# Graph attention on one core: scores dealt to row groups, transposed by TensorE, summed over heads by VectorE

## The chip, the cores and the metric

The kernel runs on one core of a Trainium2 chip. The metric is the device time of one execution in microseconds (us). The kernel before takes 5000.75 us, the median of three runs (4999.63 to 5002.16).

## What is computed

One layer of graph attention with 12,500 nodes of 128 features and 412,500 edges, followed by two layer norms. The part that the change touches is the attention score of an edge: eight heads, each with its own bias and leaky ReLU, whose mean goes into one softmax over all edges.

```python
h = node_features @ Wn + bn
q, k, v = (node_features @ W + b for W, b in ((Wq, bq), (Wk, bk), (Wv, bv)))
eh = edge_features @ We + be
attn_in = jnp.concatenate([q[src], k[tgt], eh], axis=-1)
hmid = jax.nn.leaky_relu(attn_in @ A1 + b1, SLOPE)          # 128 wide, per edge
scores = jax.nn.leaky_relu(hmid @ A2 + b2, SLOPE)           # 8 heads, per edge
w = jax.nn.softmax(scores.mean(axis=-1), axis=0)            # over all edges
out = jax.ops.segment_sum(w[:, None] * v[tgt], src, num_segments=num_nodes)
y = layernorm(h + out) * gamma + beta
result = layernorm(x + y)                                   # without gain
```

## The kernel before, in words

The edges arrive sorted by target and must be summed by source. The kernel cuts them into 403 groups of 1024 edges and the groups into six **parts** (51, 62, 73, 73, 73 and 71 groups). It does two things at once.

**Making records** (`make`, L770). For each group TensorE forms the edge's 256-wide record (key and edge terms, and the value) by one-hot products (`rows`, L878 and L884), ScalarE copies it out of PSUM (`evacuate`, L895), and POOL writes each tile of 128 records to its place in a table in HBM by an indirect DMA (L907, 3224 of them, eight to a group). The place is counted by VectorE and TensorE (L809 to L860). Records are bucketed by the block of source nodes, 98 blocks in all.

**Summing units** (`sums_of`, L1004). A unit is two blocks of one part, so there are 49 units to a part and 294 in all. A unit holds 10 tiles of 128 records in the first part, 12 in the second and 14 in the other four. The records of a part can be read only when all of the part's groups are written, so the units of part p are summed while the records of part p + 1 are made, and the 49 units of the last part after the last record is written. The order is written out by hand: `sums_of` gives every function of a unit a step, and the loop at L1625 deals the steps evenly between the pieces of `make`. Nothing is reordered afterwards: each engine runs its instructions in that order.

A unit goes through these functions. `load` (L1037) reads its records `rt` from HBM into one of six buffers. `sources` (L1059) forms the local source index `sl` on VectorE, `turn` (L1068) transposes it on TensorE, `turned` (L1075) makes bytes of it (`slT`), `put` (L1082) writes them to HBM and `spread` (L1087) reads them back to all partitions as `rowB`: two DMAs, one after the other. With `rowB`, `onehot` (L1096) makes one-hot rows of four tiles at a time, `hidden` (L1105) adds the query term by products and the record's term by transposes (L1110) in PSUM, and `sloped` and `leaky` (L1130 on ScalarE, L1134 on VectorE) leave the hidden layer in the SBUF tile `hm`, 128 features by 14 times 128 edges.

Then come the functions that the change touches. `scores` (L1141) multiplies `hm` by the 128x8 weight, padded to 32 columns, in up to four **row groups**: tiles 0 to 3 of a unit of 14 go to partitions 0 to 31 of one PSUM bank, tiles 4 to 7 to partitions 32 to 63, 8 to 11 to the third and the last two to the fourth. The fourth group is shorter, so `biased` (ScalarE, L1162) and `leaky_scores` (VectorE, L1170) work in two pieces: 96 partitions by 512 columns and 32 by 256 (96 by 384 and 32 by 128 with 10 tiles, a single 128 by 384 with 12). `heads` (L1172) sums the heads and brings the edges back to partitions in one step: four products (three with 10 or 12 tiles) with the scores as the stationary operand and a 128x4 matrix of ones, `headsum`, as the moving one. They land in the first 14 columns of a PSUM bank `psS`. `maxima` (L1186) adds the mask and takes the maximum per partition, `maximum` (L1197) brings the 128 maxima to all partitions by a product with the identity, `reference` (L1205) takes the unit's maximum, `weights` (L1216) the exponentials. `select`, `weigh` and `add` (L1224 to L1274) sum the weighted values by source in other columns of the same bank, `total` (L1276) adds them to what the earlier parts gave, and `store` writes them.

PSUM has one bank `psc`, shared by `turn` and `scores`, and two banks `psm`, one to a unit, which `total` frees. After the last unit, `closing` norms the nodes.

Of the kernel before, what the change touches and what calls it, by code (L numbers as in the profile page):

```python
# [10 lines left out]
FP = mybir.dt.float32  # L11
# [9 lines left out]
P = 128  # L21
D = 128
DE = 64
H = 8
# [423 lines left out]
def sorted_path(  # L448
# [256 lines left out]
    empties(np_)  # L705
    A2s = const.tile([D, 32], FP)
    b2_c = const.tile([P, 1], FP)
    headsum = const.tile([P, 4], FP)

    def heads_consts():  # L710

        nc.vector.memset(A2s, 0.0)
        nc.sync.dma_start(out=A2s[:, :H], in_=A2)
        nc.vector.memset(b2_c, 0.0)
        nc.vector.memset(headsum, 0.0)
        for j in range(4):
            nc.sync.dma_start(out=b2_c[32 * j : 32 * j + H, :], in_=b2)
            nc.vector.memset(headsum[32 * j : 32 * j + 32, j : j + 1], 1.0)

    def spans():  # L720

# [282 lines left out]
    def sums_of(bp):  # L1004
# [129 lines left out]
            nc.vector.tensor_tensor(hm, ph[:, : n * P], hm, op=ALU.max)  # L1134


        def slices(m):
            sw = -(-m // 4)
            return sw, [(j, min(sw, m - j)) for j in range(0, m, sw)]

        def scores(i, t0, m):  # L1141
            st = state[i]
            sw, sl = slices(m)
            hm = st["hm"].pop(t0)
            psc = pscp.tile([P, 4 * P], FP, name="psc")
            for q, (j, n) in enumerate(sl):
                nc.tensor.matmul(  # L1147
                    psc[32 * q : 32 * q + 32, : n * P], A2s, hm[:, j * P : (j + n) * P],
                    start=True, stop=True,
                )  # L1150
            full = sum(n == sw for _, n in sl)
            st["z"] = psc, [(0, 32 * full, sw)] + [
                (32 * q, 32 * q + 32, n) for q, (_, n) in enumerate(sl) if q >= full
            ]

        def biased(i):
            st = state[i]
            psc, pieces = st["z"]
            z = zp_.tile([P, 4 * P], FP, name="z")
            st["z"] = z, pieces  # L1160
            for p0, p1, n in pieces:
                nc.scalar.activation(  # L1162
                    z[p0:p1, : n * P], psc[p0:p1, : n * P], AF.Identity, bias=b2_c[p0:p1, :]
                )

        def leaky_scores(i):
            z, pieces = state[i]["z"]
            for p0, p1, n in pieces:
                zs = z[p0:p1, : n * P]
                nc.vector.scalar_tensor_tensor(zs, zs, SLOPE, zs, op0=ALU.mult, op1=ALU.max)  # L1170

        def heads(i, t0, m):  # L1172
            st = state[i]
            sw, sl = slices(m)
            if t0 == 0:
                st["psS"] = psmp.tile([P, 4 * P], FP, name="psm")
            z = st.pop("z")[0]
            for j in range(sw):
                nv = sum(n > j for _, n in sl)
                nc.tensor.matmul(  # L1180
                    st["psS"][:, t0 + j : t0 + j + (nv - 1) * sw + 1 : sw],
                    z[: 32 * nv, j * P : (j + 1) * P], headsum[: 32 * nv, :nv],
                    start=True, stop=True,
                )

        def maxima(i):  # L1186

            st, nt = state[i], plans[i][0]
            st["S"] = scp.tile([P, TM], FP, name="S")
            nc.vector.scalar_tensor_tensor(  # L1190
                st["S"][:, :nt], st["sl"][:, :nt], 0.0, st["psS"][:, :nt],
                op0=ALU.min, op1=ALU.add,
            )
            st["mx"] = scp.tile([P, 1], FP, name="mx")
# [2 lines left out]
        def maximum(i):  # L1197

            st = state[i]
            psS = st["psS"]  # L1200
            nc.tensor.matmul(
                psS[:, :P], st.pop("mx").to_broadcast([P, P]), ident, start=True, stop=True
            )

        def reference(i):  # L1205
# [549 lines left out]
```

## Time and profile before

| | |
|---|---|
| median of three runs | 5000.75 us |
| the profiled execution's own time | 4997.18 us |
| its span, first to last instruction | 4995.4 us |
| busy: TensorE (PE), VectorE (DVE) | 4185.0, 3984.1 us |
| busy: ScalarE (ACT), GpSimd (POOL) | 3260.1, 3315.9 us |
| mean granted TensorE clock | 0.906 |

PE is TensorE's products and PEld its weight loads, which run beside them; DVE is VectorE, ACT ScalarE, SP the queue that issues most DMAs. A row of the table of groups gives line, engine, operation and tiles with their shape, the count, then busy time and the mean duration in ns, and behind a bar the idle time of the engine just before such instructions with what ended it. A float32 product stands in the trace as two products and two weight loads (the 1078 products of L1180 are 2156 rows), a transpose as one. The chain of waits follows the last instruction back, at each step to what released it; its rows give start, duration and what ran.

### The profile page before, as it was taken

How to read it: one execution, taken by the hardware profiler on the slowest of the kernel's cores; microseconds unless marked ns; L12 is line 12 of the kernel's file. 1: busy time of each engine (PE TensorE's matmuls, PEld its weight loads, DVE VectorE, ACT ScalarE, POOL GpSimd, SP SyncE). 2: the span in 40 equal slices, each digit the busy share in tenths (PEclk: the TensorE clock that was granted, in tenths of full speed). 3: DMA queues.
4: the chain of work that ended last, by engine and by line, in shares of the span. 5: the costliest groups of instructions: out<-in, count | busy, mean ns of one | idle time of the engine just before them, and what ended most of it. 6: DMA issues, size and time to landing. Idle time of an engine off the chain costs nothing.

```text
span 4995.4 us, 98371 instructions
## 1 busy us (share of the span) xinstructions
PE 4185.0 (84%) x32676; PEld 3106.9 (62%) x32676; DVE 3984.1 (80%) x10117; ACT 3260.1 (65%) x8686; POOL 3315.9 (66%) x3268
## 2 busy tenths in 40 slices
PE   5665488898888888899999899999899999899980
PEld 3443366676566666577676676676677766667760
DVE  8886477788777777788888888888888888677778
ACT  3433266666566666677677677777777777677876
POOL 5777777777777777777777777777777777310002
PEclk7776588899999999999999899999999999999995
DMA  8999699998999988899899898989899999788763
GB/s 287 360 349 347 237 327 340 347 301 269 307 322 334 324 294 289 281 318 310 309 307 311 297 322 313 311 305 314 285 329 313 321 318 309 251 291 278 263 224 142
DMA packets 604241, 1505.50 MB, mean 301 GB/s; under 512 B 103587, under 2 KB 315702, under 8 KB 601929
## 3 DMA queue, kind: packets, MB, share of 16 engines
q1 hardware_dynamic: 448681, 1069.47, 64.9%
q0 software_dynamic: 154752, 429.39, 22.7%
q8 instruction: 259, 4.24, 0.3%
q14 instruction: 261, 2.14, 0.1%
q10 hardware_dynamic: 288, 0.26, 0.0%
HBM read 929.49 MB, written 608.37 MB: 308 GB/s over the span
## 4 chain that ended last, share of the span: by engine, by line
DMA 35%; PE 23%; DVE 15%; POOL 12%; issue 7%; ACT 6%; SPq 1%; ACTq 0%; DVEq 0%; POOLq 0%
DMA rtab<-rec,idx 17%; POOL rtab L907 12%; DMA rt<-rtab 8%; PE psm L1271 6%; DMA row<-slT 4%; PE ph L1119 4%; DMA rowB<-row 3%; PE pkv L884 3%; PE ph L1110 3%; ACT rec L895 2%; PE psc L1147 2%; DVE hm L1134 2%; PE pkv L878 2%; ACT ohw L1242 2%; PE psm L1180 2%
## 5 line engine op out<-in xcount | busy, mean ns | idle before, releaser
L907 POOL DMA_INDIRECT rtab<-rec,idx x3224 | 3253.2, 1009 | 1046.2 <-issue 778.6
L895 ACT ACTIVATE rec<-pkv 128x1024 f32<-128x1024 f32 x806 | 821.9, 1020 | 876.0 <-DMA rtab<-rec,idx 550.4
L1242 ACT ACTIVATE ohw<-ohs,w 128x128 f32<-128x128 bf16 x3822 | 1258.4, 399 | 44.7 <-DVE ohs L1228 34.3
L1271 PE MATMUL psm<-rt,ohw 128*128 128x128 f32 x7644 | 1160.2, 294 | 9.7 <-ACT ohw L1242 9.3
L1271 PEld LDWEIGHTS psm<-rt,ohw 128*128 128x128 f32 x7644 | 999.1, 200 | 58.7 <-ACT ohw L1242 16.8
L1130 ACT ACTIVATE hm<-ph 128x512 f32<-128x512 f32 (+1 forms) x1078 | 581.5, 539 | 403.9 <-PE ph L1119 399.8
L1119 PE MATMUL ph<-ohT,qs 128*128 128x256 bf16 (+3 forms) x4116 | 819.7, 321 | 0.0
L878 PE MATMUL pkv<-kvs,ohd 128*128 128x256 bf16 x3224 | 532.0, 292 | 263.4 <-ACT rec L895 252.8
L1134 DVE TENSOR_TENSOR hm<-ph,hm 128x512 f32<-128x512 f32 (+1 forms) x1078 | 668.4, 620 | 102.6 <-ACT hm L1130 101.4
L1110 PE MATMUL ph<-ident,rt 128*128 128x128 f32 x3822 | 628.1, 283 | 44.5 <-DVE hm L1134 43.2
L884 PE MATMUL pkv<-WeS,eat 64*128 64x128 f32 x6448 | 635.6, 320 | 0.0
L884 PEld LDWEIGHTS pkv<-WeS,eat 64*128 64x128 f32 x6448 | 469.8, 205 | 191.7 <-issue 187.3
L1099 DVE TENSOR_SCALAR ohT<-rowB,iotaP 128x512 bf16<-128x512 uint8 (+1 forms) x1078 | 518.7, 481 | 85.4 <-DMA rowB<-row 80.6
L878 PEld LDWEIGHTS <-ohd 128*128 128x128 bf16 x3224 | 317.1, 103 | 388.0 <-issue 298.2
L1110 PEld LDWEIGHTS ph<-ident,rt 128*128 128x128 f32 x3822 | 472.5, 152 | 62.0 <-DVE hm L1134 51.2
L1228 DVE TENSOR_TENSOR ohs<-iotaE,sl 128x512 bf16<-128x512 bf16 (+1 forms) x1078 | 430.0, 399 | 68.3 <-ACT ohw L1242 66.4
L1119 PEld LDWEIGHTS <-qs 128*128 128x128 bf16 x4116 | 396.0, 100 | 128.7 <-issue 5.1
L847 DVE TENSOR_TENSOR ats<-pc,oh 128x792 f32<-128x792 f32 x403 | 392.2, 973 | 86.6 <-PE pc L829 82.7
L1180 PE MATMUL psm<-headsum,z 128*128 128x4 f32 (+1 forms) x2156 | 285.7, 254 | 135.7 <-DVE part L1287 88.3
L1147 PE MATMUL psc<-hm,A2s 128*32 128x512 f32 (+3 forms) x2352 | 341.1, 545 | 65.7 <-DVE slT L1078 62.1
L858 DVE TENSOR_REDUCE pos<-ats 128x8 f32<-128x792 f32 x403 | 390.0, 968 | 4.0
L1180 PEld LDWEIGHTS psm<-headsum,z 128*128 128x128 f32 (+1 forms) x2156 | 280.0, 201 | 156.8 <-DVE part L1287 105.9
(175 smaller groups left out, 4082.3 us busy)
## 6 DMA issues: line engine op xcount, KB each, us to landing
rt<-rtab SPq DMA_DIRECT2D x196, 1820.0 KB
eat<-in_ea SPq DMA_DIRECT2D x201, 512.0 KB
rt<-rtab SPq DMA_DIRECT2D x49, 1560.0 KB
rt<-rtab SPq DMA_DIRECT2D x49, 1300.0 KB
qs<-qtab SPq DMA_DIRECT2D x294, 192.0 KB
rtab<-rec,idx POOLq DMA_INDIRECT x3224
dstb<-dtab SPq DMA_DIRECT2D x201, 256.0 KB
rtab<-empty SPq DMA_DIRECT2D x98, 520.0 KB
```

The lines of the kernel that those rows point to most:

```text
L878: nc.tensor.matmul(pk[:, h, i, :], ohd[:, t * P : (t + 1) * P], kvs, start=(i == 0), stop=False,)
L884: nc.tensor.matmul(pk[:, h, i, :D], eat[h * DE : (h + 1) * DE, (j + i) * P : (j + i + 1) * P], WeS[h * DE : (h + 1) * DE, :], start=False, ...
L895: nc.scalar.activation(rec[:, :, :, : 2 * D], pk, AF.Copy)
L907: one_tile = nc.gpsimd.indirect_dma_start(out=rtab[p % TABS][:, :], out_offset=bass.IndirectOffsetOnAxis(ap=idxs[g][:, t : t + 1], axis=0) ...
L1099: nc.vector.tensor_scalar(st["oh"][k][:, : n * P], st["rowB"][:, t0 * P : (t0 + n) * P], iotaP, None, op0=ALU.is_equal,)
L1110: nc.tensor.matmul(ph[:, j * P : (j + 1) * P], st["rt"][:, t0 + j, :D], ident, is_transpose=True, start=(j == 0), stop=False,)
L1119: nc.tensor.matmul(ph[:, cols], st["qs"][:, j0 // t, s, :], oh[:, cols], start=False, stop=(s == 2 and j1 == t0 + n),)
L1130: nc.scalar.activation(hm, state[i]["ph", k][:, : n * P], AF.Copy, scale=SLOPE)
L1134: nc.vector.tensor_tensor(hm, ph[:, : n * P], hm, op=ALU.max)
L1180: nc.tensor.matmul(st["psS"][:, t0 + j : t0 + j + (nv - 1) * sw + 1 : sw], z[: 32 * nv, j * P : (j + 1) * P], headsum[: 32 * nv, :nv], sta ...
L1242: nc.scalar.activation(ohw[:, j, :], ohs[:, :, j], AF.Copy, scale=st["w"][:, t0 + j : t0 + j + 1])
L1271: nc.tensor.matmul(st["psS"][:, (1 + u) * P : (2 + u) * P], ohw[:, j, :], st["rt"][:, t0 + j, D : 2 * D], start=(k == 0), stop=(k == t - 1),)
```

## The change

Tile t of a unit now goes to row group t mod 4 and column block t div 4, so `scores` reads every fourth tile of `hm`. Where a group has a tile less than the others, an extra product fills its last block with a copy of the group's first tile, so that the four groups are equally wide, and `biased` and `leaky_scores` work on one piece of 128 partitions. `heads` transposes each block of 128 columns against the identity, and its output now takes 32 columns of `psS` per tile. `maxima` first sums the eight heads of each tile with a reduction of VectorE that reads PSUM, and then adds the mask from SBUF. `maximum` is the same operation marked as a transpose. `headsum` goes, with its five memsets.

```diff
         def scores(i, t0, m):
             st = state[i]
-            sw, sl = slices(m)
-            hm = st["hm"].pop(t0)
+            hm = st["hm"].pop(t0).rearrange("d (t e) -> d t e", e=P)
             psc = pscp.tile([P, 4 * P], FP, name="psc")
-            for q, (j, n) in enumerate(sl):
+            to = psc.rearrange("r (j e) -> r j e", e=P)
+            w = -(-m // 4)
+            for q in range(4):
+                n = len(range(q, m, 4))
                 nc.tensor.matmul(
-                    psc[32 * q : 32 * q + 32, : n * P], A2s, hm[:, j * P : (j + n) * P],
-                    start=True, stop=True,
-                )
+                    to[32 * q : 32 * q + 32, :n, :], A2s, hm[:, q:m:4, :], start=True, stop=True
+                )
+                if n < w:
+                    nc.tensor.matmul(
+                        to[32 * q : 32 * q + 32, n:w, :], A2s, hm[:, q : q + 1, :],
+                        start=True, stop=True,
+                    )
...
         def biased(i):
...
-            for p0, p1, n in pieces:
-                nc.scalar.activation(
-                    z[p0:p1, : n * P], psc[p0:p1, : n * P], AF.Identity, bias=b2_c[p0:p1, :]
-                )
+            nc.scalar.activation(z[:, :w], psc[:, :w], AF.Identity, bias=b2_c)
 
         def leaky_scores(i):
-            z, pieces = state[i]["z"]
-            for p0, p1, n in pieces:
-                zs = z[p0:p1, : n * P]
-                nc.vector.scalar_tensor_tensor(zs, zs, SLOPE, zs, op0=ALU.mult, op1=ALU.max)
+            z, w = state[i]["z"]
+            nc.vector.scalar_tensor_tensor(
+                z[:, :w], z[:, :w], SLOPE, z[:, :w], op0=ALU.mult, op1=ALU.max
+            )
 
         def heads(i, t0, m):
...
-            for j in range(sw):
-                nv = sum(n > j for _, n in sl)
+            for j in range(-(-m // 4)):
+                k = 32 * min(4, m - 4 * j)
                 nc.tensor.matmul(
-                    st["psS"][:, t0 + j : t0 + j + (nv - 1) * sw + 1 : sw],
-                    z[: 32 * nv, j * P : (j + 1) * P], headsum[: 32 * nv, :nv],
-                    start=True, stop=True,
+                    st["psS"][:, j * P : j * P + k], z[:k, j * P : (j + 1) * P], ident[:k, :k],
+                    is_transpose=True, start=True, stop=True,
                 )
 
         def maxima(i):
...
+            nc.vector.tensor_reduce(
+                st["S"][:, :nt],
+                st["psS"].rearrange("p (t r) -> p t r", r=32)[:, :nt, :H], AX.X, ALU.add,
+            )
             nc.vector.scalar_tensor_tensor(
-                st["S"][:, :nt], st["sl"][:, :nt], 0.0, st["psS"][:, :nt],
+                st["S"][:, :nt], st["sl"][:, :nt], 0.0, st["S"][:, :nt],
                 op0=ALU.min, op1=ALU.add,
             )
...
             nc.tensor.matmul(
-                psS[:, :P], st.pop("mx").to_broadcast([P, P]), ident, start=True, stop=True
+                psS[:, :P], st.pop("mx").to_broadcast([P, P]), ident,
+                is_transpose=True, start=True, stop=True,
             )
```

The order in which the functions are called is the same. What stands on the engines is shown at three places of a unit of 14 tiles of the last part, where only sums are left. A row is a line, an operation, output <- inputs and the output's shape; a float32 product is one row here.

First TensorE at `heads`, before the change: `z` is the scores, `headsum` the matrix of ones, and the row behind them is the transposes of `hidden`.

```order
L1071 MATMUL psc<-identB,sl 14x128
L1271 MATMUL psm<-rt,ohw 128x128 x4
L1180 MATMUL psm<-headsum,z 128x4 x2
L1180 MATMUL psm<-headsum,z 128x3 x2
L1110 MATMUL ph<-ident,rt 128x128 x2
```

The same place after the change (lines have moved: L1110 is now L1107, L1271 is L1266):

```order
L1068 MATMUL psc<-identB,sl 14x128
L1266 MATMUL psm<-rt,ohw 128x128 x4
L1171 MATMUL psm<-ident,z 128x128 x3
L1171 MATMUL psm<-ident,z 128x64
L1107 MATMUL ph<-ident,rt 128x128 x2
```

Four products with few columns have become four transposes at the same place.

Second TensorE at `scores` and `maximum`, before the change, where `A2s` is the padded weight and `mx` the maxima:

```order
L1119 MATMUL ph<-ohT,qs 128x512
L1147 MATMUL psc<-hm,A2s 32x512 x3
L1147 MATMUL psc<-hm,A2s 32x256
L1201 MATMUL psm<-ident,mx 128x128
L1271 MATMUL psm<-rt,ohw 128x128 x4
```

And after the change:

```order
L1116 MATMUL ph<-ohT,qs 128x512
L1142 MATMUL psc<-hm,A2s 32x512 x2
L1142 MATMUL psc<-hm,A2s 32x384
L1146 MATMUL psc<-hm,A2s 32x128
L1142 MATMUL psc<-hm,A2s 32x384
L1146 MATMUL psc<-hm,A2s 32x128
L1195 MATMUL psm<-ident,mx 128x128
L1266 MATMUL psm<-rt,ohw 128x128 x4
```

Four products have become six, and the extra product of the third group stands ahead of the fourth group's own. `maximum` stands where it stood.

Third VectorE at `maxima`, before the change: `slT` is what `put` writes, `ohs` the one-hot of `select`, `S` the sums with the mask, and the last row is the last piece of `hm`, which the unit's scores need.

```order
L1078 TENSOR_SCALAR slT<-psc 14x128
L1228 TENSOR_TENSOR ohs<-iotaE,sl 128x128x2
L1190 SCALAR_TENSOR_TENSOR S<-sl,psm 128x14
L1195 TENSOR_REDUCE mx<-S 128x1
L1099 TENSOR_SCALAR ohT<-rowB,iotaP 128x512
L1134 TENSOR_TENSOR hm<-ph,hm 128x256
```

And after the change:

```order
L1075 TENSOR_SCALAR slT<-psc 14x128
L1223 TENSOR_TENSOR ohs<-iotaE,sl 128x128x2
L1180 TENSOR_REDUCE S<-psm 128x14
L1184 SCALAR_TENSOR_TENSOR S<-sl,S 128x14
L1189 TENSOR_REDUCE mx<-S 128x1
L1096 TENSOR_SCALAR ohT<-rowB,iotaP 128x512
L1131 TENSOR_TENSOR hm<-ph,hm 128x256
```

The reduction stands behind `turned` and ahead of the last piece of `hm`. Elsewhere on VectorE and ScalarE the second row of L1170 and of L1162 is gone from units of 10 and 14 tiles; POOL and SP have the rows that they had.

19 lines of the change are left out of this document (4 added, 15 removed).

## The prediction

> **What bounds the kernel now.** I read the page's groups first, then busy time by stage, then the chain of waits inside two stages. The stages are cut where the POOL queue starts, where the first units are summed (640), where the last record is written (4303), where the chain changes its kind (4573) and where TensorE ends (4860).
>
> ```profile
> L907 POOL DMA_INDIRECT rtab<-rec,idx x3224 | 3253.2, 1009 | 1046.2 <-issue 778.6
> L907 POOL DMA_INDIRECT rtab<-rec,idx x3224: 957/963/1824, 31.3 to 4302.8; - x190
> core 0: us, PE busy (x) PEld busy (x) DVE busy (x) ACT busy (x) POOL busy (x), PEclk, DMA share, GB/s
> 31.00:640.00 609.00, 368.36 (x2071) 245.19 (x2071) 447.56 (x992) 229.06 (x516) 447.56 (x450) 0.70 0.94 323
> 640.00:1300.00 660.00, 571.48 (x4517) 423.60 (x4517) 510.49 (x1292) 414.03 (x1101) 498.22 (x493) 0.90 0.93 315
> 1300.00:4303.00 3003.00, 2718.88 (x22135) 2035.99 (x22133) 2476.67 (x6069) 2104.06 (x5588) 2306.68 (x2283) 0.96 0.91 309
> 4303.00:4573.00 270.00, 238.52 (x1770) 180.52 (x1770) 191.55 (x513) 188.49 (x555) 30.69 (x15) 0.96 0.83 284
> 4573.00:4860.00 287.00, 277.87 (x2143) 213.99 (x2142) 221.46 (x660) 236.83 (x702) 0.00 (x0) 0.99 0.70 247
> POOL rtab L907 <- issue: 553.6, 1815, 0.3
> ```
>
> *Up to 4303 the POOL queue is the bound.* From 1300 to 4303 it issues 2283 indirect DMAs in 3003 us, one in 1.315 us: 1.010 us of work (2306.68 / 2283) and a pause of 0.30 us that no other engine ends. The longest single pause there is 0.3 us, so POOL never waits for anyone. TensorE is busy for nine tenths of that stage and still has room. A faster PE, DVE or ACT gains nothing here; only a shorter issue does. The median issue is 0.963 us and the mean 1.009, so some are lengthened.
>
> *From 4303 to 4573 a round trip of two DMAs is the bound.* The next rows are the chain of waits there (start, duration, what):
>
> ```profile
> 4406.85 0.69 DVE hm L1134
> 4407.53 0.18 DVE slT L1078
> 4407.72 0.03 DVE ohs L1228
> 4407.75 5.32 DMA row<-slT
> ...
> 4413.13 4.55 DMA rowB<-row
> ...
> 4417.71 0.03 DVE ohT L1099
> ...
> 4418.79 0.19 DVE slT L1078
> ```
>
> The byte rows of one unit go to HBM (5.32 us) and come back (4.55 us), VectorE makes the first one-hot, a piece of `hm` and then the next unit's byte rows, which go the same way: 11.26 us from one `slT` to the next, with TensorE idle in between. Nothing in that ring is changed.
>
> *From 4573 to 4860 TensorE is the bound.* It is busy for 278 of 287 us, and the chain runs through it alone:
>
> ```profile
> 4690.52 0.89 PE psm L1271 x8
> 4691.41 0.44 PE ph L1110 x4
> 4691.85 0.65 PE ph L1119 x3
> 4692.50 0.99 PE psc L1147 x5
> 4693.48 0.42 PE psm L1201 x2
> ...
> 4698.83 0.95 PE psm L1180 x8
> ...
> 4700.38 0.89 PE psm L1271 x8
> ```
>
> One unit takes 9.86 us here, of which the changed lines have 0.99 + 0.42 + 0.95. After 4860 TensorE is done and VectorE and ScalarE norm the nodes, which the change leaves alone.
>
> **The change part by part.** Units per stage come from the operation that each has once, `reference`; durations from the groups by shape and from the timeline.
>
> ```profile
> 640.00:1300.00 660.00, 13.13 (x47) 0.90 0.93 315
> 1300.00:4303.00 3003.00, 54.62 (x194) 0.96 0.91 309
> 4303.00:4573.00 270.00, 6.46 (x23) 0.96 0.83 284
> 4573.00:4860.00 287.00, 8.14 (x29) 0.99 0.70 247
> L1170 DVE SCALAR_TENSOR_TENSOR z<-z 32x256 f32<-32x256 f32 x196 | 82.8, 423 | 2.8
> L1162 ACT ACTIVATE z<-psc,b_c 32x256 f32<-32x256 f32 x196 | 91.6, 467 | 5.0
> L1209 DVE TENSOR_REDUCE m<-psm 128x1 f32<-128x128 f32 x294 | 82.6, 281 | 9.6 <-PE psm L1201 9.0
> 4648.91 0.97 PEld L1180 LDWEIGHTS psm<-headsum,z 128*128 128x128 f32 x8
> 4641.49 0.47 PEld L1110 LDWEIGHTS ph<-ident,rt 128*128 128x128 f32 x4
> 4642.78 1.06 PE L1147 MATMUL psc<-hm,A2s 128*32 128x512 f32 x8
> PEld psc L1147 <- DVE hm L1134: 45.2, 103, 2.0
> ```
>
> *`heads` on TensorE.* Four float32 products are eight passes whose weight loads set the pace, 0.97 us; four transposes of the same shape, those of L1110, have four loads in 0.47 us and stand in the chain with 0.44 against 0.95 or, elsewhere, 0.79. I take 0.40 us less per unit, between 0.35 and 0.50.
>
> *`maximum` on TensorE.* Two passes become one; one of L1110's is 0.11 us (0.44 / 4). 0.11 us less.
>
> *`scores` on TensorE.* The eight passes of today overlap: 1.06 us together. The extra products lie in the two groups that have 384 columns instead of 512, so that no group has more than 512. I cost them at nothing, hidden beside the first two groups. If they ran alone, four passes of 128 columns would add 0.45 us.
>
> *A wait that is added.* The first product of a unit's scores now reads tiles of all four pieces of `hm`; today only the last of the four products needs the last piece. Behind it in TensorE's order stand `maximum` and the next sums, and ScalarE waits for the scores. TensorE's weight loads waited 45.2 us in 103 of 294 units for `hm` before the scores. I take 0.05 us per unit, between 0 and 0.15 (45.2 / 294), since part of these waits fell on the shorter fourth group.
>
> So a unit costs TensorE 0.40 + 0.11 - 0.05 = 0.46 us less. In the last stage, 29 units, that would be 13 us if nothing else were near. But the round trip is near: with TensorE a little faster it becomes the later one.
>
> ```profile
> DVE ohT L1099 <- DMA rowB<-row: 22.3, 18, 2.9
> DVE ohT L1099 <- DMA rowB<-row: 3.7, 5, 1.2
> ```
>
> The first row is VectorE's wait for the returned rows in the stage from 4303, the second in the stage from 4573. There 5 units of 29 already wait for it. I take six tenths of the gain, 0.28 us for each of 29 units: **-8 us**, with the ends 0 and -14 (29 x 0.48). The stage before it: 0, because the ring hides whatever TensorE saves, and it is not itself shortened.
>
> *VectorE and ScalarE.* ScalarE loses 0.467 us and VectorE 0.423 us per unit of 14 tiles. The new reduction reads 112 elements per partition from PSUM; L1209 reads 128 in 0.281 us, so I put it at 0.27. Neither engine ends a wait that counts: in the last stage they are busy for 221 and 237 of 287 us, in the ring neither piece stands between `ohT` and `slT`. The reduction stands ahead of the last piece of `hm`; without room behind it, it would cost 0.27 us per unit of the last stage, 8 us, which is the whole of its gain.
>
> *POOL's issues.* This is the term with the least known price. A timeline from the long stage:
>
> ```profile
> 3046.38 1.11 DVE L1170 SCALAR_TENSOR_TENSOR z<-z 96x512 f32<-96x512 f32 x2
> 3046.87 1.03 POOL L907 DMA_INDIRECT rtab<-rec,idx  x1 [0.32 <-issue]
> 3048.21 0.96 POOL L907 DMA_INDIRECT rtab<-rec,idx  x1 [0.31 <-issue]
> ```
>
> The issue beside the two pieces of `z` took 1.03 us, the next one 0.96. If the pieces lengthen an issue by 0.07 us, the smaller one, 0.42 of 1.11 us, has 0.03 of it, or all of it at most. 193 smaller pieces (245 less the 52 of the last two stages) stand before 4303: -6 to -14 us, and I take -10. The reduction, in 241 units, may lengthen issues as well: 0 to 0.03 us each, 0 to +7, and I take +3 because it reads PSUM. Together **-7 us**, on a stage where POOL is the bound and every ns of an issue counts. No added row stands on POOL or SP.
>
> The Trainium skill's page "SBUF — State Buffer", in its box on the trap that VectorE blocks DMA, says that an operation of VectorE which uses both ports keeps GpSimd from writing descriptors until it ends. By that rule an issue would lose up to the whole 0.42 us per small piece; the row above has 0.07 us for both pieces, so the trace bears it out in direction and not in size. The sum by the rule stands among the rivals.
>
> *Sum.* -7 - 8 = -15 on the profiled execution's 4997.18 us (span 4995.4): 4982. The median of the runs is 3.6 us above that execution, so **4986 us**.
>
> **The rivals.**
> - *Nothing comes of it.* The round trip takes over the last stage at once, and the issues don't change: 4998 to 5001. For it: 18 of 23 units wait for the ring in the stage before. Against it: 24 of 29 don't in the last.
> - *All of it comes.* 29 x 0.48 = 14 and 14 on POOL: 4973. For it: ScalarE's and VectorE's pieces also go. Against it: the ring.
> - *VectorE locks POOL out for a whole piece.* 193 x 0.42 = 81 us less, 4912 with the last stage's 8. Against it: the mean issue is only 0.046 us above the median. That is the mechanism of the page named above.
> - *Slower: the reduction lengthens POOL's issues more than the piece did.* At 0.07 us in each of 241 units, 17 us, against 6 that the piece gives back, with no gain in the last stage: 5012. It decides from 0.06 us per reduction on. Against it: L1209 also reads PSUM, and the issues' median stays at the floor.
> - *Slower: TensorE's clock sinks.* 19 passes of a unit instead of 14 are transposes. At the 0.90 granted from 640 to 1300 the last stage's 9.4 us would be 10.3: 29 x 0.5 = 14 us more, 5008 with POOL's 7 less. It decides at about 0.94. Against it: the clock is 0.99 in a stage with 14 transposes per unit.
>
> The Trainium skill's page "TensorE: Matmul & The Clock Gate", Part 4, says that transposes do not count as activity for the clock gate; by that rule the last rival would be the likely one. The 0.99 of that stage speaks against it.
>
> **How the numbers follow.** Forecast 0.42, nothing 0.30, all 0.17, the lock 0.02, the two slower ones 0.05 and 0.04. A difference of 0.2% (10 us) is about what a measurement can tell from no change. Faster by more: 0.38 of the forecast's 0.42 (it reaches to -6), 0.17 and 0.02: 0.57. Slower by more: 0.09. Within: 0.34, the rest of the forecast and the case that nothing comes. The range goes from -30 (14 + 14 and 2) to +5, which leaves out the lock and the slower ones: 4970 to 5006.
>
> **What would show it.** Right: the mean issue of POOL falls by 2 to 5 ns with the median unchanged; the last record lands near 4296; `heads` has some 0.45 us in the chain; a unit takes 9.5 to 9.6 us in the last stage, with more waits of VectorE for `rowB`; the stage before it keeps 11 us. Wrong: the scores take clearly more than 0.99 us in the chain (the extra products run alone), TensorE waits there for `hm` in most units, the clock in the last stage is under 0.94, or issues of 1.0 us and more become more frequent.

## The result and the profile after

The changed kernel takes 4995.38 us (median; 4988.27 to 5001.56 in 12 runs), the kernel before 5000.94 us beside it on the same chip. The ratio is 0.9986 with a 95% interval of 0.9978 to 0.9995: 5.6 us, or 0.14%, less. In a second comparison the ratio of the same two kernels was 0.9993 (0.9984 to 1.0003), and there the kernel before, run once more against itself, came out at 0.9995 (0.9986 to 1.0004). So the gain is clear of noise in the first comparison alone, and even there it is about a third of the 15 us that were forecast.

The profiled execution takes 4998.21 us (span 4996.5), against 4997.18 (4995.4) before, so the two profiled executions show no gain at all. What they show is where time was saved and where it was given back. Line numbers of the change are 3 to 5 lower than before: L907 is L904, L1099 is L1096, L1134 is L1131, L1147 is L1142, and L1271 is L1266.

POOL's issues, from the page's groups (busy us, mean ns, then idle time before them):

```profile
L904 POOL DMA_INDIRECT rtab<-rec,idx x3224 | 3247.6, 1007 | 1046.9 <-issue 799.1
```

and the same line by itself (shortest, median and longest in ns, first and last start):

```profile
L904 POOL DMA_INDIRECT rtab<-rec,idx x3224: 955/963/1760, 31.2 to 4297.8; - x190
```

The mean fell from 1009 to 1007 ns, the median stayed at 963, and the last record is issued at 4297.8 instead of 4302.8: 5 us earlier.

Busy time in the same stages as before (PE, PEld, DVE, ACT, POOL, then clock, DMA share, GB/s):

```profile
640.00:1300.00 660.00, 548.42 (x4524) 402.72 (x4522) 499.18 (x1286) 392.79 (x1054) 495.56 (x490) 0.90 0.92 314
1300.00:4303.00 3003.00, 2612.11 (x21777) 1937.65 (x21777) 2445.99 (x6116) 2009.62 (x5439) 2302.98 (x2282) 0.96 0.90 309
4303.00:4573.00 270.00, 236.01 (x1750) 173.78 (x1750) 187.73 (x520) 178.13 (x535) 29.66 (x14) 0.94 0.84 283
4573.00:4860.00 287.00, 268.74 (x2106) 202.65 (x2106) 212.66 (x649) 221.09 (x671) 0.00 (x0) 0.98 0.70 245
```

In the last of them TensorE was busy for 277.87 us and is busy for 268.74: it has 9 us of idle time more, and nothing ends earlier. From the end of the last record to the end of the span it is 697.7 us, where it was 691.6. The chain of waits in that stage (start, duration, what) says why:

```profile
4638.44 0.68 DVE hm L1131
4639.12 0.20 DVE slT L1075
...
4639.33 5.75 DMA row<-slT
...
4645.15 5.10 DMA rowB<-row
...
4650.27 0.04 DVE ohT L1096
...
4650.68 0.68 DVE hm L1131
4651.36 0.19 DVE slT L1075
...
4653.12 0.96 PE psc L1142 x5
4654.08 0.13 PE psc L1146 x3
4654.20 0.25 PE psm L1195
```

This is the round trip of the byte rows that bound the stage before: out to HBM in 5.75 us, back in 5.10, then the first one-hot, a piece of `hm`, the next byte rows. It takes a quarter of this stage's chain (13.8% for `row`, 11.2% for `rowB`); before, `row` had 1.9%. Before, the chain ran through TensorE for most of the stage, but not alone, as the prediction had it: loads of records stand in it with 5.9%. The next rows are one such load and, from an undisturbed unit, `maximum` and `heads`:

```profile
4666.62 8.43 DMA rt<-rtab
...
4703.35 0.42 PE psm L1201 x2
...
4708.69 0.79 PE psm L1180 x8
```

After the change, the waits from 4573 to 4860 (us in total, times, longest) show both ends of it:

```profile
DVE sl L1060 <- DMA rt<-rtab: 35.6, 25, 3.3
PEld psc L1142 <- DVE hm L1131: 16.7, 28, 0.9
DVE ohT L1096 <- DMA rowB<-row: 16.2, 9, 2.8
PEld ph L1107 <- DVE hm L1131: 10.6, 10, 1.9
```

VectorE's wait for the returned rows grew from 3.7 us in 5 units to 16.2 in 9, and TensorE now waits for `hm`, ahead of the scores and ahead of the transposes.

### The profile page after: what moved, and what is told of

It is laid out like the page before. It is cut to its first block, busy times and chain, and to the rows that moved or that the text cites. A ratio compares the mean times of both kernels' runs of the same rounds, so it can differ in the third digit from the quotient of the medians.

```text
span 4996.5 us, 97387 instructions
## 1 busy us (share of the span) xinstructions
PE 4037.1 (81%) x32284; PEld 2966.2 (59%) x32284; DVE 3933.0 (79%) x10161; ACT 3120.0 (62%) x8441; POOL 3310.0 (66%) x3268
## 4 chain that ended last, share of the span: by engine, by line
DMA 41%; DVE 16%; PE 14%; POOL 14%; issue 8%; ACT 7%; SPq 1%; ACTq 0%; DVEq 0%; POOLq 0%
DMA rtab<-rec,idx 20%; POOL rtab L904 14%; DMA rt<-rtab 8%; DMA row<-slT 5%; DMA rowB<-row 4%; PE psm L1266 3%; ACT rec L892 3%; DVE hm L1131 3%; PE ph L1116 2%; ACT ohw L1237 2%; PE ph L1107 2%; PE pkv L881 2%; PE psc L1142 2%; DVE pos L855 1%; DVE ohT L1096 1%
## 5 line engine op out<-in xcount | busy, mean ns | idle before, releaser
L904 POOL DMA_INDIRECT rtab<-rec,idx x3224 | 3247.6, 1007 | 1046.9 <-issue 799.1
L1266 PE MATMUL psm<-rt,ohw 128*128 128x128 f32 x7644 | 1149.9, 293 | 2.9 <-ACT ohw L1237 2.7
L1266 PEld LDWEIGHTS psm<-rt,ohw 128*128 128x128 f32 x7644 | 998.5, 201 | 47.8 <-ACT ohw L1237 6.8
L1131 DVE TENSOR_TENSOR hm<-ph,hm 128x512 f32<-128x512 f32 (+1 forms) x1078 | 668.9, 620 | 145.3 <-ACT hm L1127 142.8
L1107 PE MATMUL ph<-ident,rt 128*128 128x128 f32 x3822 | 635.2, 285 | 58.4 <-DVE hm L1131 56.2
L1096 DVE TENSOR_SCALAR ohT<-rowB,iotaP 128x512 bf16<-128x512 uint8 (+1 forms) x1078 | 506.8, 470 | 109.1 <-DMA rowB<-row 108.8
L1107 PEld LDWEIGHTS ph<-ident,rt 128*128 128x128 f32 x3822 | 451.0, 146 | 97.0 <-DVE hm L1131 69.6
L1142 PE MATMUL psc<-hm,A2s 128*32 128x384 f32 (+2 forms) x2352 | 311.3, 562 | 176.9 <-DVE hm L1131 165.1
L1060 DVE SCALAR_TENSOR_TENSOR sl<-mask,rt 128x14 bf16<-128x14 bf16 (+2 forms) x294 | 52.3, 178 | 348.6 <-DMA rt<-rtab 347.7
L820 DVE TENSOR_SCALAR ohd<-dstb,node 128x1024 bf16<-128x1024 uint8 x403 | 306.6, 761 | 0.0
```

The source lines that it names most:

```text
L904: one_tile = nc.gpsimd.indirect_dma_start(out=rtab[p % TABS][:, :], out_offset=bass.IndirectOffsetOnAxis(ap=idxs[g][:, t : t + 1], axis=0) ...
L1096: nc.vector.tensor_scalar(st["oh"][k][:, : n * P], st["rowB"][:, t0 * P : (t0 + n) * P], iotaP, None, op0=ALU.is_equal,)
L1107: nc.tensor.matmul(ph[:, j * P : (j + 1) * P], st["rt"][:, t0 + j, :D], ident, is_transpose=True, start=(j == 0), stop=False,)
L1266: nc.tensor.matmul(st["psS"][:, (1 + u) * P : (2 + u) * P], ohw[:, j, :], st["rt"][:, t0 + j, D : 2 * D], start=(k == 0), stop=(k == t - 1),)
```

## The experiments

All numbers that recur are in one table. "Issues" are POOL's from 1300 to 4290; "tail" goes from the end of the last issue to the end of the span. The units of the last part are counted by the operation that each has once, `refs` (L1264 before, L1259 in the change): first the 20 units up to the one that stands 31 places from the end, then the 28 units after it. The ratio is to the kernel before on the same chip.

| kernel | ratio (95%) | issues | last issue at | tail | us per unit, 20 units | next 28 |
|---|---|---|---|---|---|---|
| before | | 2273 | 4302.8 | 691.6 | 10.98 | 9.98 |
| before_again | 0.9995 (0.9986 to 1.0004) | 2274 | 4308.2 | 694.0 | 11.04 | 10.01 |
| the change | 0.9986 (0.9978 to 0.9995) | 2275 | 4297.8 | 697.7 | 11.32 | 10.02 |
| change_again | 0.9993 (0.9984 to 1.0003) | 2277 | 4296.9 | 694.6 | 11.18 | 10.01 |
| one_piece | 0.9992 (0.9981 to 1.0002) | 2276 | 4304.0 | 690.3 | 10.89 | 10.00 |
| two_pieces | 1.0034 (1.0022 to 1.0046) | 2260 | 4330.7 | 690.7 | 11.29 | 9.79 |
| ring_before | 1.0371 (1.0351 to 1.0391) | 2210 | 4407.8 | 793.7 | 12.72 | 12.33 |
| ring_after | 1.0179 (1.0165 to 1.0194) | 2257 | 4329.9 | 762.0 | 12.29 | 11.74 |
| ring3_before | 1.0049 (1.0035 to 1.0062) | 2250 | 4337.9 | 688.3 | 11.06 | 9.89 |
| ring3_after | 1.0020 (1.0011 to 1.0030) | 2255 | 4326.4 | 683.1 | 11.35 | 9.54 |
| last_before | 0.9998 (0.9984 to 1.0011) | | 5429.2 | 701.3 | 11.43 | 9.87 |
| last_after | 0.9956 (0.9941 to 0.9971) | | 5402.3 | 689.5 | 11.35 | 9.61 |
| last_full | 0.9960 (0.9944 to 0.9977) | | 5421.8 | 686.7 | 11.21 | 9.48 |
| four_reduces | 1.0018 (1.0004 to 1.0031) | | 5423.5 | 704.3 | 11.37 | 10.04 |

The last four ran on a chip where the kernel before takes 6130 us. In these four POOL waits 720 to 860 us for ScalarE's records (L896, L893 in the change), against 48 us in the kernel before elsewhere, and the mean granted clock is 0.84 instead of 0.91; why is not known. Of these four only what comes after the last record is read.

**The theory** after the result: up to the last record the change gains what the smaller piece of `z` took from POOL; after it, TensorE saves 0.43 us per unit (undisturbed units take 9.70 us before and 9.27 in the change) and the round trip of the byte rows takes it back. **The rivals**: the dealt scores, which wait for the last piece of `hm`, eat TensorE's gain; the transposes save nothing; what moved at the last record is chance.

### The dealing and the single piece alone

The products with `headsum`, the old `maxima` and the product in `maximum` come back:

```diff
-                k = 32 * min(4, m - 4 * j)
+                nv = min(4, m - 4 * j)
                 nc.tensor.matmul(
-                    st["psS"][:, j * P : j * P + k], z[:k, j * P : (j + 1) * P], ident[:k, :k],
-                    is_transpose=True, start=True, stop=True,
+                    st["psS"][:, 4 * j : 4 * j + nv], z[: 32 * nv, j * P : (j + 1) * P],
+                    headsum[: 32 * nv, :nv], start=True, stop=True,
```

> Only the dealing and the single piece of z are kept; heads sums by products with the ones, maxima adds the mask to PSUM and maximum is a product, as before. Theory (what the change gains up to the last record comes from VectorE's smaller piece of z, what TensorE gains after it is taken back by the ring of two DMAs): the last record lands at 4296 to 4299 (before 4302.8, change 4297.8), the stretch after it takes 690 to 692 us as in the kernel before, TensorE ends the last stage's chain with about 9.8 us per unit; 4993 to 4997 in all. Rival 1 (the 5 us up to the last record are chance, or come of something other than the piece): last record at 4302 or later, 5000. Rival 2 (the dealing itself, by which the scores wait for the last piece of hm, eats the gain of the tail): the stretch after the last record is 6 us or more longer than before, 5000 or more.

The last record is issued at 4304.0, which is rival 1's number and not the theory's; the tail of 690.3 us is the theory's, so rival 2 falls: dealing the tiles costs the tail nothing. The first point needs more care. From 1300 to 4290, where POOL is the bound:

```profile
1300.00:4290.00 2990.00, 2675.32 (x22295) 2066.81 (x22653) 2397.18 (x5914) 2013.26 (x5423) 2295.21 (x2276) 0.96 0.91 310
```

These are 2276 issues, as many as in the two executions of the change (2275 and 2277), against 2273 and 2274 before. So the piece may give back 2 to 3 issues there, 3 to 4 us, which is little beside the 1 or 2 issues between executions of one kernel; the time of the last record also holds what happened up to 1300, which differs by as much or more.

### The second piece put back

```diff
-            nc.vector.scalar_tensor_tensor(
-                z[:, :w], z[:, :w], SLOPE, z[:, :w], op0=ALU.mult, op1=ALU.max
-            )
+            for p0 in (0, 64):
+                zs = z[p0 : p0 + 64, :w]
+                nc.vector.scalar_tensor_tensor(zs, zs, SLOPE, zs, op0=ALU.mult, op1=ALU.max)
```

(and `biased` on ScalarE the same way)

> The change with biased and leaky_scores in two pieces of 64 partitions, so that VectorE and ScalarE have a second operation of 512 columns per unit again, while the transposes and the reduction stay. Theory: POOL's issues are lengthened again, the mean issue is at or over the 1009 ns of before, the last record lands at 4303 to 4309, all else as in the change; 5001 to 5007. Rival 1 (the piece does nothing to POOL): last record at 4298, 4995.

```profile
L904 POOL DMA_INDIRECT rtab<-rec,idx x3224 | 3269.8, 1014 | 1057.4 <-issue 788.9
```

The mean issue is 1014 ns and 2260 of them fit between 1300 and 4290, 16 fewer than in the change. The direction is the theory's, and the size is over it: 16 x 1.315 = 21 us for 194 units, 0.11 us for each second piece (0.69 us in a unit of 14 tiles). The small one had given 3 to 4 us. Counted one by one in the traces, the issues of this stretch that overlap an operation of VectorE on `z` take 1.070 us in the mean in the change (235 of them) and 1.085 here (332), all others 1.003 and 1.005. So the longer issues go with VectorE's pieces. That the pieces cause it is not shown: ScalarE has a second operation per unit here as well, and no run has the one without the other.

One more thing differs from the change, against what was expected:

```profile
L1262 ACT ACTIVATE refs<-ref x29: 203/203/205, 4581.0 to 4855.2; 128x2 f32<-128x2 f32 x29
DVE ohT L1096 <- DMA rowB<-row: 3.1, 2, 1.8
```

The first row is `refs` of the last 28 units and of the one ahead of them, the second the wait for `rowB` from 4573 to 4860. It is 3.1 us here, and the last 28 units take 274.2 us, 6 less than in the change, although VectorE and ScalarE have more to do. So where the round trip happens not to be late, part of TensorE's gain appears.

### The round trip broken, first attempt

In both kernels, for units of 14 tiles, `turn` one step earlier and the three behind it two:

```diff
-            do(s0 - turn_at, turn, i)
-            do(s0 - turn_at + 1 + e, turned, i)
-            do(s0 - turn_at + 1 + e, put, i)
-            do(s0 - turn_at + 3 + 2 * e, spread, i)
+            d = 2 if nk > 3 else 0
+            do(s0 - turn_at - d // 2, turn, i)
+            do(s0 - turn_at + 1 + e - d, turned, i)
+            do(s0 - turn_at + 1 + e - d, put, i)
+            do(s0 - turn_at + 3 + 2 * e - d, spread, i)
```

> The kernel before with turn one step earlier and turned, put and spread two steps earlier for units of 14 tiles, so that the next unit's byte rows stand on VectorE ahead of the first one-hot, and the round trip of the two DMAs no longer hangs on the first one-hot of the unit ahead. Theory: from 4303 to 4573 a unit takes 9.7 to 9.9 us instead of 11.3, 24 units by 1.4 us, 30 to 36 us less; in the last stage little, 9.7 per unit; 4964 to 4971. Rival (TensorE or the waits for hm set the pace there too and the ring is only the later of two near ends): 10 us or less are gained, over 4988.

> The change with the same earlier turn, turned, put and spread. Theory (the ring took back what TensorE gained): all 52 units after the last record go at the pace that the change has when it isn't held up by the ring, 9.2 to 9.4 us, where the kernel before with the same edit has 9.7: 20 to 25 us less than that kernel, 4942 to 4950, and some 45 to 50 us less than the change. Rival 1 (the scores' wait for the last piece of hm, which the dealing added, eats the gain of TensorE): the pace per unit is that of the kernel before with the same edit within 0.1 us, the two kernels differ by the 5 us of POOL alone. Rival 2 (the transposes and the reduction save TensorE nothing): as rival 1, with heads at over 0.8 us in the chain.

Both became slower, by 3.7% and 1.8%, which no theory had. The waits of ring_before from 4573 to 4860:

```profile
DVE sl L1063 <- DMA rt<-rtab: 90.0, 24, 5.4
...
DVE ohT L1099 <- DMA rowB<-row: 1.0, 1, 1.0
```

The wait for the returned rows is gone, as meant, and another took its place: the load of a unit's records (`rt`). Two steps earlier, `put` of one unit stands on SP ahead of the load of a later one, so the load waits with `put` for `slT`. In the chain of ring_before the load starts 0.46 us behind `slT`:

```profile
4640.42 0.19 DVE slT L1078
4640.61 0.34 DVE ohs L1228
4641.07 8.17 DMA rt<-rtab
4649.27 0.18 DVE sl L1063
```

`sl` then waits for the 8 us of the load. This pair says nothing on the theory, only that the edit has to leave SP's order alone.

### The round trip broken, loads left in place

```diff
-            do(s0 - turn_at + 1 + e, turned, i)
-            do(s0 - turn_at + 1 + e, put, i)
-            do(s0 - turn_at + 3 + 2 * e, spread, i)
+            d = int(nk > 3)
+            do(s0 - turn_at + 1 + e - d, turned, i, late=-d)
+            do(s0 - turn_at + 1 + e - d, put, i)
+            do(s0 - turn_at + 3 + 2 * e - d, spread, i)
```

> The kernel before, with turned, put and spread one step earlier for units of 14 tiles and turned ahead of the rest of its step on VectorE; turn and the order of the loads on SP stay. So the next unit's byte rows stand ahead of the first one-hot on VectorE, and no row write stands ahead of a load of records. Theory: the round trip of the two DMAs no longer hangs on the first one-hot, a unit from 4303 on takes 9.7 to 9.9 us as TensorE sets it, and the stretch after the last record takes 655 to 665 us instead of 691.6. Rival (the loads of records, for which VectorE's sl waits 1.2 us in nearly every unit, are the next ring and no later than the first): the stretch stays over 680 us.

> The change with the same edit. Theory (the ring of the two DMAs took back what TensorE gained): 9.2 to 9.4 us per unit, the stretch after the last record 15 to 25 us shorter than in the kernel before with the same edit, 632 to 648 us. Rival 1 (the dealt scores' wait for the last piece of hm eats TensorE's gain): within 5 us of the kernel before with the same edit. Rival 2 (the loads of records bind next): both stay over 680 us.

The last 28 units separate the theories. One row each, of the operation that a unit has once: before, the change, ring3_before, ring3_after.

```profile
L1264 ACT ACTIVATE refs<-ref x29: 203/203/204, 4548.7 to 4828.0; 128x2 f32<-128x2 f32 x29
```

```profile
L1259 ACT ACTIVATE refs<-ref x29: 203/203/205, 4549.3 to 4829.8; 128x2 f32<-128x2 f32 x29
```

```profile
L1264 ACT ACTIVATE refs<-ref x29: 203/204/205, 4585.1 to 4861.9; 128x2 f32<-128x2 f32 x29
```

```profile
L1259 ACT ACTIVATE refs<-ref x29: 203/203/205, 4578.8 to 4845.9; 128x2 f32<-128x2 f32 x29
```

28 units take 279.3 us before and 280.5 in the change; with the round trip broken they take 276.8 and 267.1. The change alone gains nothing, breaking the trip alone gains 2.5, both together gain 12. So with the trip broken the change is worth 10 us here (276.8 against 267.1). The waits of ring3_after from 4573 to 4860:

```profile
DVE sl L1060 <- DMA rt<-rtab: 47.6, 28, 3.0
PEld psc L1142 <- DVE hm L1131: 12.9, 29, 0.7
...
DVE ohT L1096 <- DMA rowB<-row: 2.3, 4, 0.8
...
PE psc L1142 <- DVE hm L1131: 0.7, 3, 0.3
```

The wait for `rowB` is down to 2.3 us. The weight loads of the scores still wait for `hm`, but the products behind them only for 0.7 us in 29 units: the added wait exists and is nearly hidden, so the dealt scores don't eat TensorE's gain. Nor do the transposes save nothing, since an undisturbed unit takes 9.27 us against 9.70.

The other expectation of this pair failed. The tails of 688.3 and 683.1 us are 5 us apart, where 15 to 25 were expected: that is at rival 1's line of 5, and both are over 680, as rival 2 has it. In the 20 units before the last 28 the pace stayed at 11.06 and 11.35 us, so the change loses 6 us there of the 10. From 4400 to 4450 the chain of ring3_before is, by line:

```profile
by line: DMA rt<-rtab 55.7%; DMA row<-slT 33.5%; DVE hm L1134 6.0%; DVE z L1170 3.9%; issue 2.8%; DVE ohs L1228 2.2%; DVE part L1287 2.1%; DVE ohT L1099 1.4%; SPq L1354 1.4%; SPq L1090 1.3%; DVE m L1209 1.2%; DVE sl L1063 1.1%; SPq L1353 0.
```

There the loads of records, for which VectorE's `sl` waits, take the larger part, and the write of the byte rows still a third: rival 2 of ring3_after was right, for this stage.

The edit also cost 30 us before the last record. POOL's groups in ring3_before:

```profile
L907 POOL DMA_INDIRECT rtab<-rec,idx x3224 | 3283.5, 1018 | 1051.0 <-issue 792.1
```

The same operations in another order (`turned` earlier on VectorE, `put` and `spread` earlier on SP) make the mean issue 9 ns longer. Counted in the traces from 1300 to 4290, all of it lies in the issues that overlap `ohT` on VectorE: some 775 of them take 1.039 us in the mean before and 1.080 in ring3_before, the others 0.996 in both. Why these grow longer was not tried.

### Both kernels once more

> The change itself once more, for a second profile. Theory (POOL's issues are shorter by some 1.5 ns each, 3.5 us from 1300 to the last record; what differs up to 640, where no unit is summed yet, is chance): 1.314 to 1.315 us per issue from 1300 to 4290, and the stretch after the last record 695 to 700 us. Rival (the whole difference of the last record is chance): 1.316 us per issue.

> The kernel before once more, for a second profile. Theory: 1.316 us per issue from 1300 to 4290, and 690 to 693 us after the last record. Rival (chance): 1.315 or less per issue, or a stretch after the last record of over 695 us.

The last issue is at 4296.9 in the change and 4308.2 before, so the distance is 5 and 11 us in the two pairs. From 1300 to 4290 there are 2277 issues against 2274: 1.313 against 1.315 us each (2990 / 2277 and 2990 / 2274). Both are about 1 ns under what was expected, and the kernel before stands at the line that was drawn between theory and chance. Between the two kernels lie 2.5 issues in the mean, 3.3 us, with 1 or 2 issues between executions of one kernel. The rest of the distance is there by 1300 and can't be told from chance with two executions each. Nor can the 3.3 us be called shown: the nearest executions of the two kernels are 1 issue apart. The tails, 694.6 and 694.0, both lie just outside what was expected, and the 6 us by which the change's tail was longer in the first pair are 0.6 in this one.

### The round trip broken in the last part alone

```diff
-            d = int(nk > 3)
+            d = int(units[i][0] == NP - 1)
```

> The kernel before with the earlier turned, put and spread in the units of the last part alone, so that nothing moves while POOL is the bound. Theory: the last record stays at 4303 to 4309, the stretch after it is 688 us (688.3 with the edit everywhere, 691.6 and 694.0 without it), since TensorE needs 9.70 us per unit in the last stage with or without the ring. Rival: the last record moves as with the edit everywhere (4338).

> The change with the same edit in the last part alone. Theory (the ring took back what TensorE gained, and the 30 us that the edit cost everywhere were POOL's issues, not the tail): the last record at 4297 to 4300, the stretch after it at 683 us (697.7 and 694.6 without the edit), 9.3 to 9.5 us per unit in the last stage, so some 12 us under the change and 14 to 18 us under the kernel before, a ratio near 0.9965. Rival 1: the tail needs what the edit did in the earlier parts, 694 us or more. Rival 2: the last record moves to 4327.

On this chip the last issue came at 5429.2 and 5402.3, so where it stands against 4303 can't be said. After it: 701.3 us in the kernel before, 689.5 in the change, 9.87 and 9.61 us per unit in the last 28. They were expected 5 us apart (688 and 683) and are 12 apart, 7.5 of these in the last 28 units; the levels are 13 and 6 us over what was expected. The ratio of 0.9956 is the lowest in the table, but the change itself was not timed on this chip (0.9986 and 0.9993 elsewhere). And the 12 us of the tail are 0.2% of 6130 us; the rest of the 0.44% lies before the last record, where POOL waits for others on this chip, and is not explained.

### 128 rows in every transpose of `heads`

```diff
-                k = 32 * min(4, m - 4 * j)
+                k = P
```

> The same, and heads transposes 128 rows for every block, also where only 64 hold scores (the fill columns are transposed with them). Theory (the last transpose with 64 rows among those with 128 makes TensorE drain twice, 0.2 us): heads takes 0.45 us instead of 0.63 and a unit of the last stage 9.0 to 9.2 us where TensorE sets the pace, 3 to 7 us less after the last record. Rival (VectorE's wait for the loads of records or the chain of ohT, hm and scores sets the pace by then): heads is shorter but a unit still takes 9.3 us, the stretch 682 to 684 us.

Weight loads of `heads` and of the transposes behind it in last_after (start, duration):

```profile
5811.69 0.36 PEld L1171 LDWEIGHTS psm<-ident,z 128*128 128x128 f32 x3
5812.22 0.14 PEld L1171 LDWEIGHTS psm<-ident,z 64*128 64x128 f32 x1 [0.17 <-issue]
5812.42 0.20 PEld L1107 LDWEIGHTS ph<-ident,rt 128*128 128x128 f32 x2
```

and in last_full:

```profile
5811.58 0.42 PEld L1171 LDWEIGHTS psm<-ident,z 128*128 128x128 f32 x4
5811.96 0.25 PEld L1107 LDWEIGHTS ph<-ident,rt 128*128 128x128 f32 x2
```

The load with 64 rows stands 0.17 us idle first, and so late that L1107 begins 0.73 us after `heads` did instead of 0.38. The undisturbed unit falls from 9.27 to 9.03 us, as expected, the mean of 28 from 9.61 to 9.48, and the tail by 2.8 us, a little less than was expected. The ratio doesn't tell it from the kernel without this edit.

### The reduction four times

```diff
-            nc.vector.tensor_reduce(
+            for _ in range(4):
+                nc.vector.tensor_reduce(
```

> The change with the reduction over heads done four times, three of them for nothing. It adds 0.78 us per unit on VectorE, about as much as the second piece of z in the run with two pieces (0.69 us), but reads PSUM. By the prediction's estimate (3 us for one) POOL's last record is 9 us later than in the change, 4307. Rival 1 (VectorE's time counts, whatever it reads): 0.78/0.69 of the 26 to 33 us that the second piece cost, 4328 or later. Rival 2 (an operation that reads PSUM lengthens no issue): 4298. After the last record up to 0.78 us more per unit of the last stages where VectorE has no room, 0 to 40 us.

The price on POOL can't be read on this chip, where POOL isn't the bound. After the last record the 28 units take 10.04 us each, as in the change (10.02). The chain of waits (start, duration, what) shows the four in it:

```profile
5751.39 0.19 DVE S L1181
...
5751.61 0.29 DVE S L1181
...
5751.92 0.28 DVE S L1181
...
5752.23 0.28 DVE S L1181
...
5752.91 0.39 DVE ohT L1096
5753.31 0.34 DVE hm L1131
...
5753.69 0.95 PE psc L1142 x5
```

A unit now takes 9.90 us almost every time, where the change has 9.27 and 11 by turns. So the reduction does stand on the way to the scores, and three more of it set the pace. One alone costs an undisturbed unit nothing that shows: in ring3_after such a unit takes 9.27 us, which is 9.70 less what TensorE saves.

## Why the prediction was right or wrong

*What bounds the kernel.* From 1300 to 4303 it held: POOL's pauses stay short, and the time moves with the length of an issue (two_pieces, ring3). For the next stage the round trip was right, but it isn't alone: with it broken the loads of records bind at the same 11 us. For the last stage "TensorE is the bound", read from one unit of the chain, was half of it, see below.

*POOL, -7 us.* The last record came 5 and 11 us earlier in the two pairs, so the sum looks right, but that is in part luck: at most 3 to 4 us of it can be laid to the change. The terms were -10 for the small piece and +3 for the reduction. The kernel without the reduction fits as many issues between 1300 and 4290 as the two executions with it, so the reduction costs nothing that these runs resolve, and the piece gives 3 to 4 us at most, not 10. The estimate split the 0.07 us of one pair of pieces between two operations by their time. The run with two pieces speaks against this measure: a second piece of 512 columns, 1.6 times as long as the small one, cost six times as much, with ScalarE's second operation in the price.

The Trainium skill's box on the trap that VectorE blocks DMA (page "SBUF — State Buffer") has an issue stand still for an operation that uses both ports. Whether the operation on `z` is one, no run here shows, and the prediction took it so without a sign. The largest price that was measured is 0.11 us for a piece of 0.69 us, so in the mean POOL lost far less than a whole piece here.

*TensorE, 0.46 us per unit.* The sum held, since two terms were off in opposite directions. The undisturbed unit goes from 9.70 to 9.27 us, 0.43 less. In the clean chain of ring3_after:

```profile
4730.78 0.53 PE psm L1171 x4
...
4733.98 0.89 PE psc L1142 x5
4734.87 0.12 PE psc L1146 x3
4734.99 0.25 PE psm L1195
```

An undisturbed `heads` took 0.79 us before (the 0.95 of the prediction's lines is a disturbed one) and takes 0.53: it saves 0.26, and 0.40 was forecast. What is missing goes with the transpose of 64 rows, which the prediction priced like the others: with 128 rows in each, a unit takes another 0.24 us less. `maximum` takes 0.25 instead of 0.42 and saves 0.17, where 0.11 was forecast. The scores take 1.01 instead of 0.99, so the extra products are hidden. The wait for the last piece of `hm` costs the products 0.7 us in 29 units with the trip broken, 0.02 us each; 0.05 was taken. In the change itself the weight loads wait for `hm` in 28 of 29 units, the sign that the prediction named for being wrong, though the products behind them wait in 11 alone, 4.4 us in all.

*The last stage, -8 us: this is the step that failed.* "I take six tenths of the gain" should have been none: 28 units took 279.3 us before and 280.5 after. The argument was that 24 of 29 units don't wait for the round trip. But a wait is counted only where it was the last one at that moment. A sign was in the numbers of before: an undisturbed unit took 9.70 us there and the mean of 28 was 9.98, so something beside TensorE already set part of the pace. Breaking the trip alone took a third of that gap (9.89); the rest goes with other waits, the loads of records among them. In the change undisturbed units of 9.27 us alternate with units of 11 or more, and the mean stays at 10.0. The pair of ring3 shows that the gain was real: with the trip broken the same TensorE work gives 10 us of the 13 that the prediction had "if nothing else were near". (Its end of -14 takes 0.48 us per unit where its terms give 0.46; nothing hangs on it.)

Why 1.8 KB take 5 us and more each way is not measured here. The Trainium skill's page "Perfetto Trace Analysis", in its section on HWDGE DMA instructions, says that a DMA's semaphore waits until its last write is confirmed, which can be surprisingly long for a target in HBM. The 5.75 us of `row`, which is written to HBM, would fit that; the 5.10 us of `rowB`, which is written to SBUF, are not covered by it.

*The stage before, 0.* The trip did hide what TensorE saved, but the stage didn't keep its 11 us: 20 units took 10.98 and 11.04 us each before, 11.32 and 11.18 in the change, some 5 us in all. That is as much as POOL gained. It is not the trip (11.06 and 11.35 with it broken), nor the dealing or the single piece (10.89 in one_piece). It goes with the transposes and the reduction (11.29 in two_pieces), though not on the chip of the last four runs (11.43 and 11.35); which of them, and how, stays open.

*The sum.* In the mean of two profiled executions each: -8 at the last record, +5 in the 20 units, +1 in the 28 and -2 ahead of and behind these, together -5 (4999.3 to 4994.5 us of span). The forecast had -15. The measured time lies in the range from 4970 to 5006 us, but that range also holds the rival by which nothing comes of the change, so the time bears out neither against the other.

*The rivals.* "Nothing comes of it", with 0.30, is the nearest. The round trip took over the last stage at once, as it said. The clock didn't sink: 0.98 in the last stage. The Trainium skill's rule that transposes don't count for the clock gate ("TensorE: Matmul & The Clock Gate", Part 4) doesn't show in a stage where 19 passes of a unit are transposes; the unit's other passes stand between them, so these runs don't test the rule itself. POOL's issues didn't lengthen, and VectorE didn't lock it out.

## What to carry to other kernels

Ahead of pricing a gain on the engine that seems to bound a stage, compare the stage's mean pace with that of a unit that nothing disturbs; a gap between them (here 9.98 against 9.70 us) says that something else already acts. It doesn't say what, nor that it takes the whole gain (a gap as large, 9.54 against 9.27, is left where most of the gain came through), so break the suspect in both kernels and compare. When such a ring is broken, watch what the moved DMA passes on its queue: here an edit that put a small write ahead of a big load cost 3.7%. And as the edit that helped the last stage cost 30 us before it, try such an edit only in the stage that gains.

## What the runs showed that was not expected

- One transpose of 64 rows among those of 128 costs TensorE 0.24 us (9.27 against 9.03 us per unit). It starts 0.17 us late, and so does the work behind it.
- A second piece of `z` per unit (0.69 us on VectorE, with one on ScalarE) cost POOL 0.11 us per unit, one of 0.42 us next to nothing; merely another order of the same operations cost 9 ns per issue, 30 us in all, and all of that in issues beside `ohT`.
- Chips differ by more than any edit here: on one, the kernel before takes 6130 us instead of 5001. There POOL pauses for ScalarE's records, while what comes after the last record takes about as long as elsewhere (701 us in last_before, 688 in ring3_before, which has the same last part).
